# A second half product of each projection in seven block products, and the sums of h in one buffer, in a two-layer graph kernel on one core

## The chip, the cores and the metric

The kernel runs on one core of a Trainium2 chip. The metric is the device time of the whole kernel in microseconds (us), the median of several runs. Before the change it is 1522.22 us, the median of 3 runs (1521.25 to 1522.27). A core has five engines with a queue of instructions each: TensorE (PE; its weight loads are shown apart as PEld), VectorE (DVE), ScalarE (ACT), GpSimd (POOL) and SyncE (SP, which here issues the DMAs).

## What is computed

x is 128 x 128 x 512 (items, nodes, features), adj 128 x 128, all in fp32. Two layers follow each other; both are normalised ahead and added to x:

```python
h = relu(layernorm(x))
# layer 0: A = adj h, C = adj h + b;  max over n of relu(A[n'] + (C - A)[n]), so that
# what is left is relu(max_n A + b): one number for each item and node
x = x + layer0(h)
h = relu(layernorm(x))              # a number per node does not change a layernorm over features
q = h @ Wq + bq;  k = h @ Wk + bk;  v = h @ Wv + bv      # 8 heads of 64
w = softmax(q k^T / 8 + (0 where adj != 0, else -1e9))
x = x + w @ v
```

## The kernel before

**Groups.** The 128 items are worked on in 32 groups of four. The projections q, k and v of a group are products of 512 x 512 by 512 x 512 (four items of 128 nodes side by side). One turn of the main loop over g does, in this order on TensorE: `apply(g-1)` (weights by v, L600), `scores(g)` (q by k, L570), then the projection v of group g, and q and k of group g+1. Between their products stand the adjacency products of layer 0 (`adjacency`, L327) of later items. Everything else is put between these by hand: each projection is a list of steps, `part`, and `todo[s]` names what is issued right after step s. No scheduler reorders anything (`manual_schedule`); each engine does its instructions in the order in which the code issues them.

**A projection in seven products.** The class `Products` does a projection by a Strassen-Winograd scheme: weights and h are cut into quarters (a11 to a22, b11 to b22), four sums of weight quarters (s1 to s4, made once) and four of h quarters (t1 to t4, `h_sum`, L345, on VectorE for every group) are formed, and seven products of half size take the place of eight: p1 = a11 b11, p2 = a12 b21, p3 = s4 b22, p4 = a22 t4, p5 = s1 t1, p6 = s2 t2, p7 = s3 t3. Each is four matmuls of 128 x 128 weights by 256 columns into one PSUM bank (`mm`, L421). ScalarE copies p1 out with the bias (`biased`); VectorE adds p6 and p7 to it (u, L469, u3), and adds u and u3 to the banks of p5, p4 and p3 (`add`, L442), which gives the four quarters of the result. p2 is accumulated in the bank of p1 (bank a), which ScalarE copies to the first quarter, `dst(0, 0)`.

**Two of the seven in blocks.** In all projections but v of the first and last group and the k that is made ahead of the loop, p4 and p3 are done by the same scheme once more. `block_views` cuts their operands into blocks of 128; `h_blocks` (GpSimd, L359) makes four block sums of t4 and of b22 for each group, `weight_blocks` once those of a22 and s4. Each of the two products is then seven block products of 128 x 128 weights by 128 columns (`block_mm`, L487). Three of these go straight into the banks of p6/p7 and p5; four (numbers 1, 5, 6, 7) go to a scratch bank, 6, and are added into u by `more` (VectorE, L490). `p43a` does blocks 1 and 5, after p7; `p43b` does 6, the three direct ones and 7, after p5, and the last two adds.

**The steps of a turn.** Slots 0 to 5 are v (p1, p6, p2, p7 + p43a, p5, p43b), 6 to 11 are q, 12 to 17 k. The sums of h for group g+1 (`h_sum`) are in slots 0, 1, 2, 2 in a buffer of two (`hs`, pool `proj`), the block sums (`h_blocks`) in slots 5 and 6. `next_norms` places the normalisation of the next items: `norm` (bn_stats L279, aggregate L280, add eps L282 on VectorE, the power and a product on GpSimd, L284 and L286), `norm_end` (ScalarE, L289), `blocks` (32 x 32 transposes on VectorE, L302), `move` (16 DMAs that complete the transposition) and `add_bv` (GpSimd, L295). GpSimd also masks the exponentials (`mask`, L582) and adds the residual (L630).

What a step issues after its slot is two lines of the loop:

```python
for s, ps_ in enumerate(part):
    for p in ps_:
        p()
    for f, *args in todo[s]:
        f(*args)
```

Of the kernel before, what the change touches and what calls it, by code (L numbers as in the profile page):

```python
# [45 lines left out]
F32 = mybir.dt.float32  # L46
# [6 lines left out]
P = 128  # L53
G = 4
H, HD = 8, 64
# [112 lines left out]
def tile_adj_preln_d2(  # L168
# [14 lines left out]
    B, D, N = x.shape  # L183
# [4 lines left out]
    const = ctx.enter_context(tc.tile_pool(name="const", bufs=1))  # L188
# [1 line left out]
    W = {n: const.tile([P, NC, N], F32, name=f"w{n}_sb") for n in "qkv"}  # L190
    WS = {n: const.tile([P, 4, 2, N // 2], F32, name=f"s{n}_sb") for n in "qkv"}

    WB = {n: const.tile([P, 2, 4, P], F32, name=f"ss{n}_sb") for n in "qkv"}
    b0_sb = const.tile([P, 1], F32, name="b0_sb")
    bq_sb = const.tile([P, NC], F32, name="bq_sb")
    bk_sb = const.tile([P, NC], F32, name="bk_sb")
# [10 lines left out]
    def fast(ctx):  # L207
        xpool = ctx.enter_context(tc.tile_pool(name="xpool", bufs=7))
        proj = ctx.enter_context(tc.tile_pool(name="proj", bufs=2))
        one = ctx.enter_context(tc.tile_pool(name="one", bufs=1))  # L210
# [6 lines left out]
        X, HN, TB, HT, HB, H2, QT, KT, C, AMAX, WA, RSTD, NMR, PR = ({} for _ in range(14))  # L217

        def bank(k):

            return ps.tile([P, 512], F32, name=f"bk{k}")
# [109 lines left out]

        def h_quarters(g):
            t = HT[g]
            hs = proj.tile([P, 4, 2, 2, D], F32, name="hs")
            HB[g] = dict(
                b11=t[:, 0:2, 0:2], b12=t[:, 2:4, 0:2], b21=t[:, 0:2, 2:4], b22=t[:, 2:4, 2:4],
                **{f"t{k + 1}": hs[:, k] for k in range(4)},
            )
# [7 lines left out]

        def h_blocks(g, k):

            if k == 0:
                H2[g] = one.tile([P, 2, 4, D], F32, name="h2")  # L350
            b = HB[g]["b22 t4".split()[k]].rearrange("p t c d -> p c t d")
            t = H2[g][:, 1 - k]

            for o, x, y in (
                (t[:, 0:2], b[:, :, 1], b[:, 0]),
                (t[:, 2], b[:, 1, 1], t[:, 0]),
                (t[:, 3], b[:, 1, 0], t[:, 2]),
            ):
                nc.gpsimd.tensor_tensor(o, x, y, op=ALU.subtract)  # L359

        def weight_blocks(eng, n):

            for k in range(2):
                a = WA[n]["a22 s4".split()[k]].rearrange("p c (o f) -> p o c f", o=2)
                s = WB[n][:, k]
                for o, x, op, y in (
                    (s[:, 0], a[:, 1, 0], ALU.add, a[:, 1, 1]),
                    (s[:, 2], s[:, 0], ALU.subtract, a[:, 0, 0]),
                    (s[:, 1], a[:, 0, 0], ALU.subtract, a[:, 1, 0]),
                    (s[:, 3], a[:, 0, 1], ALU.subtract, s[:, 2]),  # L370
                ):
                    eng.tensor_tensor(o, x, y, op=op)
# [19 lines left out]
        class Products:  # L392
# [78 lines left out]
            def block_views(self):  # L471

                self.wa = [
                    WA[self.n][k].rearrange("p c (o f) -> p o c f", o=2) for k in ("a22", "s4")
                ]
                self.hb = [
                    HB[self.g][k].rearrange("p t c d -> p c t d") for k in ("t4", "b22")
                ]
                self.scr = bank(6).rearrange("p (m k d) -> p m k d", m=2, k=2)
                o_t = "(o d) -> p {} o t d" if self.n == "v" else "(t d) -> p {} o t d"  # L480
                r = "t" if self.n == "v" else "o"
                self.ub = self.u.rearrange(f"p k {r} " + o_t.format("k"), d=D)
                self.bk = lambda x: x.rearrange(f"p {r} " + o_t.format(""), d=D)

            def block_mm(self, out, w, h, start=False):
                lhs, rhs = (h, w) if self.n == "v" else (w, h)
                nc.tensor.matmul(out, lhs, rhs, start=start, stop=True, skip_group_check=True)  # L487

            def more(self, to, what):
                nc.vector.tensor_tensor(to, to, what, op=ALU.add)  # L490

            def p43a(self):

                self.block_views()
                s, t = WB[self.n], H2[self.g]
                for k in range(2):
                    self.block_mm(
                        self.scr[:, 0, k], self.wa[k][:, 0, 0], self.hb[k][:, 0, 0], start=k == 0
                    )
                for k in range(2):  # L500
                    self.block_mm(self.scr[:, 1, k], s[:, k, 0], t[:, k, 0])
                self.more(self.ub[:, :, 0, 0], self.scr[:, 0])
                for o in range(2):
                    self.more(self.ub[:, :, o, 1], self.scr[:, 1])
# [5 lines left out]

            def p43b(self):

                s, t, u, scr = WB[self.n], H2[self.g], self.ub, self.scr
                bc = [self.bk(self.b), self.bk(self.c)]
                for k in range(2):
                    self.block_mm(scr[:, 0, k], s[:, k, 2], t[:, k, 2])
                self.more(u[:, :, 0, 1], scr[:, 0])
                for k in range(2):
                    a, b = self.wa[k], self.hb[k]
                    self.block_mm(bc[k][:, 0, 0], a[:, 0, 1], b[:, 1, 0])  # L520
                    self.block_mm(bc[k][:, 0, 1], s[:, k, 3], b[:, 1, 1])
                    self.block_mm(bc[k][:, 1, 0], a[:, 1, 1], t[:, k, 3])
                for k in range(2):
                    self.block_mm(scr[:, 0, k], s[:, k, 1], t[:, k, 1])
                for i in range(2):
                    self.more(u[:, :, 1, i], scr[:, 0])
                self.add(self.dst(1, 0), self.b, self.u[:, 0])
                self.add(self.dst(0, 1), self.c, self.u[:, 1])

# [114 lines left out]
        def next_norms(m):  # L644

            return {
                0: [(norm_end, m, False), (norm_end, m + 1, False)],
                4: [(blocks, m)],
                6: [(blocks, m + 1), (move, m + 1), (add_bv, m), (add_bv, m + 1)], 7: [(adjacency, m)],
                8: [(norm, m + 2), (norm_end, m + 2)],  # L650
                12: [(norm, m + 3), (norm_end, m + 3), (adjacency, m + 1)],
                13: [(blocks, m + 2)],
                14: [(blocks, m + 3), (move, m + 3), (adjacency, m + 2)],
            }

        with tc.manual_schedule():
# [31 lines left out]
            k = Products(0, "k")  # L688
# [12 lines left out]
            for g in range(NG):  # L701
                b = g * G
# [2 lines left out]
                scores(g)  # L705
                part = []
                for p in [Products(g, "v")] + [Products(g + 1, n) for n in "qk" if g + 1 < NG]:
                    part += [[p.p1], [p.p6], [p.p2]]
                    if p.n == "v" and g in (0, NG - 1):
                        part += [[p.p7], [p.p5], [p.p4, p.p3]]  # L710
                    else:
                        part += [[p.p7, p.p43a], [p.p5], [p.p43b]]
                todo = {s: [] for s in range(len(part))}

                def add(s, *what):
# [2 lines left out]
                m = b + 2 * G  # L718
                if g + 1 < NG:
                    if g > 0:  # L720
                        for i in range(G):
                            residual(b - G + i, nc.gpsimd)
                    if m < B:
                        norm(m)
                        norm(m + 1)
                    if 0 < g < NG - 1:
                        add(0, adjacency, m - 1)
                    for k, s in enumerate((0, 1, 2, 2) if g > 0 else (3, 3, 4, 5)):
                        add(s, h_sum, g + 1, k)
                    for k, s in enumerate((5, 6)):  # L730
                        add(s, h_blocks, g + 1, k)
                    if g + 2 < NG:
                        for s, l in next_norms(m).items():
                            for what in l:
                                add(s, *what)
                    else:
                        add(6, count, 0, b)
                    eng = nc.gpsimd if m < B else nc.vector
                    at = (8, 9, 9, 10, 10, 13, 14, 15) if m < B else (4, 8, 8, 12, 12, 13, 14, 14)
                    for k, s in enumerate(at):  # L740
                        add(s, mask, eng, b + k // 2, k % 2)
                    if g + 2 < NG:
                        add(0, load, 2 * g + 5)
                    if g + 3 < NG:
                        add(8, load, 2 * g + 6)
                else:
                    for k, s in enumerate((0, 0, 0, 0, 2, 2, 3, 4)):
                        add(s, mask, nc.vector, b + k // 2, k % 2)
                    for i, s in enumerate((0, 0, 0, 1)):
                        add(s, residual, b - G + i)  # L750
# [13 lines left out]
            g = NG - 1  # L764
# [9 lines left out]
    with ExitStack() as c:  # L774
        fast(c)
# [35 lines left out]
```

## Time and profile before

The span of the profiled execution is 1519.2 us; the granted TensorE clock is 0.998 of full speed on average.

| engine | busy us | share | instructions |
|---|---|---|---|
| TensorE, matmuls | 1504.1 | 99% | 12909 |
| TensorE, weight loads | 1325.6 | 87% | 12909 |
| VectorE | 1023.2 | 67% | 2187 |
| ScalarE | 507.3 | 33% | 970 |
| GpSimd | 844.4 | 56% | 968 |

A middle group takes 46.75 us, and the groups are alike. In one of them, v takes 12.91 us of TensorE, q 12.62, k 13.57 (adjacency products included) and apply with scores 7.65; VectorE is busy for 7.71, 7.77, 8.96 and 7.18 of these.

Each matmul of fp32 shows as two instructions with two weight loads. Since matmuls are pipelined and their ends are modelled, a matmul's duration in the profile says less than the distance between the starts of two that follow each other. On the other engines an instruction's duration is what was measured, and one that follows without a wait starts a little before the end of the one ahead. A line of the timeline is: start, length, engine, line and operation, out<-in, partitions x elements and type, number of instructions merged; in brackets the idle time ahead of it and what ended it. A line of the groups is: line, engine, operation, out<-in, shapes, number, then busy us and mean ns of one, then idle us ahead of it and what ended it.

### The profile page before, as it was taken

The page shows a single profiled execution, that of the slowest core. Times are in us where ns is not written, and L with a number is a line of the kernel's source. Part 1 is how long each engine was busy: PE and PEld are TensorE (multiplying, and loading weights), DVE is VectorE, ACT ScalarE, POOL GpSimd, SP SyncE. Part 2 cuts the span into 40 slices and gives each one's busy share as a digit, 9 for nine tenths or more (in the row PEclk, how much of TensorE's full clock was granted, in tenths as well). Part 3 has the DMA queues.
Part 4 walks back from the last instruction along what each step waited for, and adds up shares of the span by engine and source line. Part 5 has one row for each costly group of instructions (what it writes and reads, how often), then busy time and mean ns, then how long its engine had stood idle before and what let it go on. Part 6 is the DMA issues. An engine that isn't in the chain of part 4 may idle for free.

```text
span 1519.2 us, 33036 instructions
## 1 busy us (share of the span) xinstructions
PE 1504.1 (99%) x12909; PEld 1325.6 (87%) x12909; DVE 1023.2 (67%) x2187; ACT 507.3 (33%) x970; POOL 844.4 (56%) x968
## 2 busy tenths in 40 slices
PE   8999999999999999999999999999999999999997
PEld 6888888888889888888888888888988888888886
DVE  6666666666666767666666666666676766666666
ACT  4333323333243332333332333324333233333232
POOL 5675656556565555654565655656555565456520
PEclk9999999999999999999999999999999999999999
DMA  5223222223222232222322222322223222222201
GB/s 170 58 65 80 59 65 74 65 76 75 52 73 67 73 83 43 76 66 74 80 58 65 75 65 76 73 54 73 66 73 84 43 76 76 64 80 57 52 32 58
DMA packets 307807, 105.32 MB, mean 69 GB/s; under 512 B 273153, under 2 KB 273281, under 8 KB 307649
## 3 DMA queue, kind: packets, MB, share of 16 engines
q1 hardware_dynamic: 307328, 102.84, 26.3%
q8 instruction: 104, 1.70, 0.5%
q14 instruction: 55, 0.44, 0.1%
q0 software_dynamic: 176, 0.27, 0.1%
q10 hardware_dynamic: 144, 0.07, 0.0%
HBM read 37.03 MB, written 33.55 MB: 46 GB/s over the span
## 4 chain that ended last, share of the span: by engine, by line
PE 99%; DVE 0%; DMA 0%; POOL 0%; ACT 0%; DVEq 0%; issue 0%
PE bk L421 55%; PE bk L487 19%; PE bk L600 8%; PE bk L570 8%; PE bk L327 7%; PE bk L546 1%; PE bk L321 0%; DMA xp<-in_x_dram 0%; DVE o L618 0%; ACT o L289 0%; DVE live L639 0%; DVE st L279 0%; DVE RS L617 0%; DVE o L630 0%; DVEq L776 0%; POOL rstd L284 0%
## 5 line engine op out<-in xcount | busy, mean ns | idle before, releaser
L630 POOL TENSOR_TENSOR o<-xp,o 128x512 f32<-128x512 f32 x122 | 151.1, 1268 | 312.7 <-DVE o L618 269.4
L582 POOL TENSOR_TENSOR w<-w,live 128x512 f32<-128x512 f32 x240 | 297.6, 1272 | 0.0
L490 DVE TENSOR_TENSOR u<-u,bk 128x256 f32<-128x256 f32 x552 | 205.7, 414 | 115.4 <-PE bk L487 111.3
L578 ACT ACTIVATE w<-bk 128x512 f32<-128x512 f32 x256 | 128.8, 625 | 345.6 <-PE bk L570 345.6
L295 POOL TENSOR_TENSOR xp<-xp,bv_sb 128x512 f32<-128x512 f32 x128 | 161.1, 1269 | 59.5 <-ACT hn L289 58.6
L421 PEld LDWEIGHTS bk<-hs,sk_sb 128*128 128x128 f32 x768 | 143.6, 190 | 44.7 <-issue 29.4
L421 PE MATMUL bk<-hs,sk_sb 128*128 128x256 f32 x768 | 181.3, 379 | 0.0
L421 PE MATMUL bk<-sv_sb,hs 128*128 128x256 f32 x768 | 181.2, 379 | 0.0
L421 PE MATMUL bk<-hs,sq_sb 128*128 128x256 f32 x744 | 175.8, 379 | 0.0
L421 PEld LDWEIGHTS bk<-sv_sb,hs 128*128 128x128 f32 x768 | 143.6, 190 | 31.1 <-issue 14.3
L328 DVE TENSOR_REDUCE amax<-bk 128x1 f32<-128x512 f32 x128 | 88.2, 689 | 105.4 <-PE bk L327 102.5
L359 POOL TENSOR_TENSOR h<-hT 128x256 f32<-128x256 f32 x31 | 22.6, 728 | 238.2 <-PE bk L487 233.8
L421 PEld LDWEIGHTS bk<-hs,sq_sb 128*128 128x128 f32 x744 | 138.9, 190 | 17.7
L469 DVE TENSOR_TENSOR u<-bk,u 128x512 f32<-128x512 f32 x95 | 65.8, 692 | 116.7 <-PE bk L421 114.6
L289 ACT ACTIVATE hn<-xp,nmr,rstd 128x512 f32<-128x512 f32 x124 | 100.8, 813 | 104.8 <-POOL nmr L286 104.8
L327 PE MATMUL bk<-hn,adjT 128*128 128x512 f32 x248 | 126.6, 592 | 0.0
L600 PE MATMUL bk<-v,w 128*64 128x65 f32 x4096 | 126.5, 222 | 0.0
L600 PEld LDWEIGHTS bk<-v,w 128*64 128x64 f32 x4096 | 122.1, 137 | 4.1 <-issue 0.3
L421 PE MATMUL bk<-wv_sb,hT 128*128 128x256 f32 x512 | 124.3, 386 | 0.0
L570 PE MATMUL bk<-qT,kT 64*128 64x128 f32 x2048 | 122.9, 275 | 0.0
L421 PE MATMUL bk<-hT,wk_sb 128*128 128x256 f32 x512 | 121.2, 380 | 0.0
L570 PEld LDWEIGHTS bk<-qT,kT 64*128 64x128 f32 x2048 | 116.8, 188 | 2.5 <-issue 0.3
(149 smaller groups left out, 2575.1 us busy)
## 6 DMA issues: line engine op xcount, KB each, us to landing
out_dram<-o SPq DMA_DIRECT2D x128, 256.0 KB, 2.0
xp<-in_x_dram SPq DMA_DIRECT2D x62, 512.0 KB, 3.9
hT<-tb SPq DMA_DIRECT2D x992, 32.0 KB, 1.9
xp<-in_x_dram SPq DMA_DIRECT2D x4, 256.0 KB, 4.4
wq_sb<-in_L_gnn_Wq_dram SPq DMA_DIRECT2D x2, 512.0 KB, 8.2
wk_sb<-in_L_gnn_Wk_dram SPq DMA_DIRECT2D x2, 512.0 KB, 9.8
wv_sb<-in_L_gnn_Wv_dram SPq DMA_DIRECT2D x2, 512.0 KB, 10.5
bv_sb<-in_L_gnn_bv_dram POOLq DMA_DIRECT2D x1, 256.0 KB, 6.7
```

Source lines behind the costliest of these rows:

```text
L289: nc.scalar.activation(HN[m], x_of(m), AF.Relu, scale=RSTD[m], bias=NMR[m])
L295: nc.gpsimd.tensor_tensor(x_m, x_m, bv_sb, op=ALU.add)
L327: nc.tensor.matmul(pa, adjT, HN[m], start=True, stop=True)
L328: nc.vector.reduce_max(AMAX[g][:, i : i + 1], pa, axis=AX.X)
L421: nc.tensor.matmul(bank[:, r, :], lhs, rhs, start=first and r == 0 and c == 0, stop=r == 1 and c == 1, skip_group_check=True,)
L487: nc.tensor.matmul(out, lhs, rhs, start=start, stop=True, skip_group_check=True)
L490: nc.vector.tensor_tensor(to, to, what, op=ALU.add)
L570: nc.tensor.matmul(psc[j][:, f, :], KT[g][r, f, i * D : (i + 1) * D], QT[g][r, f, i * D : (i + 1) * D], start=True, stop=True,)
L578: nc.scalar.activation(w[:, j], psc[j], AF.Exp, scale=HD ** -0.5)
L582: eng.tensor_tensor(w[:, j], w[:, j], live_h, op=ALU.mult)
L600: nc.tensor.matmul(pav[r, c : c + HE], w[:, h % 2, h // 2, r], V[:, i, h, :], start=True, stop=True,)
L630: eng.tensor_tensor(y, x_of(b), y, op=ALU.add)
```

## The change

p2 is done in seven block products too, by the same scheme as p4 and p3, in the projections that use blocks. For that:

- `weight_blocks` makes block sums of a12 as well, once; `h_blocks` those of b21, for each group, in a tile of its own for each of the three operands.
- p2 becomes three steps. `p2a`, in place of p2: blocks 1 and 5 go to the two quarters `sum2` and `five` of a spare bank (2 for q, else 5), the three direct ones into bank a; ScalarE copies bank a to `dst(0, 0)` as before, and VectorE adds `sum2` and `five` into it (`more2`). `p2b`, after p7: block 6 into `sum2`, and one sum. `p2c`, after p43a: block 7 into `sum2`, and one sum.
- `hs` has one buffer in place of two (this makes room for the new tiles). The sums for group g+1 then can't be written while v of group g reads the old ones, so `h_sum` moves to slots 5, 5, 6, 6, and `h_blocks` to 5 (b21, b22) and 6 (t4).
- The last sums of v (`p43c`) are issued at slot 6, ahead of q's p1, behind the first two of these.
- `blocks` of the next two items move from slots 4 and 6 to 1 and 2, their `move` from 6 to 5.

It is for TensorE: four matmuls of 256 columns become seven of 128.

```diff
-    WB = {n: const.tile([P, 2, 4, P], F32, name=f"ss{n}_sb") for n in "qkv"}
+    WB = {n: const.tile([P, 3, 4, P], F32, name=f"ss{n}_sb") for n in "qkv"}
...
-            hs = proj.tile([P, 4, 2, 2, D], F32, name="hs")
+            hs = one.tile([P, 4, 2, 2, D], F32, name="hs")
...
-            b = HB[g]["b22 t4".split()[k]].rearrange("p t c d -> p c t d")
-            t = H2[g][:, 1 - k]
+            b = HB[g]["t4 b22 b21".split()[k]].rearrange("p t c d -> p c t d")
+            t = H2[g, k] = one.tile([P, 4, D], F32, name=f"h2{k}")
...
+            def p2a(self):
+
+                self.block_views()
+                x = bank(2 if self.n == "q" else 5)
+                self.sum2, five = x[:, 0:D], x[:, D : 2 * D]
+                self.block(self.sum2, 2, 1)
+                self.block(five, 2, 5)
+                self.blocks_in(self.bk(self.a), 2)
+                self.biased(self.dst(0, 0), self.a, 0)
+                self.more2(0, 0, self.sum2)
+                self.more2(slice(0, 2), 1, five)
+
+            def p2b(self):
+                self.block(self.sum2, 2, 6)
+                self.more2(0, 1, self.sum2)
+
+            def p2c(self):
+                self.block(self.sum2, 2, 7)
+                self.more2(1, slice(0, 2), self.sum2)
...
-                4: [(blocks, m)],
-                6: [(blocks, m + 1), (move, m + 1), (add_bv, m), (add_bv, m + 1)], 7: [(adjacency, m)],
+                1: [(blocks, m)], 2: [(blocks, m + 1)],
+                5: [(move, m + 1)], 6: [(add_bv, m), (add_bv, m + 1)], 7: [(adjacency, m)],
...
-                    part += [[p.p1], [p.p6], [p.p2]]
                     if p.n == "v" and g in (0, NG - 1):
-                        part += [[p.p7], [p.p5], [p.p4, p.p3]]
+                        part += [[p.p1], [p.p6], [p.p2], [p.p7], [p.p5], [p.p4, p.p3]]
                     else:
-                        part += [[p.p7, p.p43a], [p.p5], [p.p43b]]
+                        part += [
+                            [p.p1], [p.p6], [p.p2a], [p.p7, p.p2b, p.p43a, p.p2c], [p.p5],
+                            [p.p43b, p.p43c],
+                        ]
+                        if p.n == "v":
+                            late = part[-1].pop()
+                    if p.n == "q" and g > 0:
+                        part[6].insert(0, late)
...
-                    for k, s in enumerate((0, 1, 2, 2) if g > 0 else (3, 3, 4, 5)):
+                    for k, s in enumerate((5, 5, 6, 6)):
                         add(s, h_sum, g + 1, k)
-                    for k, s in enumerate((5, 6)):
+                    for k, s in ((2, 5), (1, 5), (0, 6)):
                         add(s, h_blocks, g + 1, k)
```

More of the change, by code (lines that the diff above doesn't have):

```diff
@@ L347, in h_blocks @@
         def h_blocks(g, k):
-            if k == 0:
-                H2[g] = one.tile([P, 2, 4, D], F32, name="h2")
-            b = HB[g]["b22 t4".split()[k]].rearrange("p t c d -> p c t d")
-            t = H2[g][:, 1 - k]
+            b = HB[g]["t4 b22 b21".split()[k]].rearrange("p t c d -> p c t d")
+            t = H2[g, k] = one.tile([P, 4, D], F32, name=f"h2{k}")
             for o, x, y in (
@@ L361, in weight_blocks @@
         def weight_blocks(eng, n):
-            for k in range(2):
-                a = WA[n]["a22 s4".split()[k]].rearrange("p c (o f) -> p o c f", o=2)
+            for k in range(3):
+                a = WA[n]["a22 s4 a12".split()[k]].rearrange("p c (o f) -> p o c f", o=2)
                 s = WB[n][:, k]
@@ L473, in block_views @@
                 self.wa = [
-                    WA[self.n][k].rearrange("p c (o f) -> p o c f", o=2) for k in ("a22", "s4")
+                    WA[self.n][k].rearrange("p c (o f) -> p o c f", o=2)
+                    for k in ("a22", "s4", "a12")
                 ]
                 self.hb = [
-                    HB[self.g][k].rearrange("p t c d -> p c t d") for k in ("t4", "b22")
+                    HB[self.g][k].rearrange("p t c d -> p c t d") for k in ("t4", "b22", "b21")
                 ]
-                self.scr = bank(6).rearrange("p (m k d) -> p m k d", m=2, k=2)
+                self.s = WB[self.n]
+                self.t = [H2[self.g, k] for k in range(3)]
                 o_t = "(o d) -> p {} o t d" if self.n == "v" else "(t d) -> p {} o t d"
@@ L487, in block_mm, with blocks_in, block @@
                 nc.tensor.matmul(out, lhs, rhs, start=start, stop=True, skip_group_check=True)
+            def blocks_in(self, bank, k):
+                a, b, s, t = self.wa[k], self.hb[k], self.s[:, k], self.t[k]
+                self.block_mm(bank[:, 0, 0], a[:, 0, 1], b[:, 1, 0])
+                self.block_mm(bank[:, 0, 1], s[:, 3], b[:, 1, 1])
+                self.block_mm(bank[:, 1, 0], a[:, 1, 1], t[:, 3])
+            def block(self, out, k, m):
+                if m == 1:
+                    self.block_mm(out, self.wa[k][:, 0, 0], self.hb[k][:, 0, 0], start=k != 1)
+                else:
+                    e = {5: 0, 6: 2, 7: 1}[m]
+                    self.block_mm(out, self.s[:, k, e], self.t[k][:, e])
@@ L489, in more, with more2 @@
             def more(self, to, what):
                 nc.vector.tensor_tensor(to, to, what, op=ALU.add)
-            def p43a(self):
[L494 to L501, printed above, removed]
+            def more2(self, o, t, what):
+                d = self.dst(0, 0)
+                if self.n == "v":
+                    d = d.rearrange("p t (o h) d -> p o t h d", o=2)
+                    what = what.rearrange("p (h d) -> p h d", d=HD)
+                else:
+                    d = d.rearrange("p o (t d) -> p o t d", t=2)
+                to = d[:, o, t]
+                if len(to.shape) > len(what.shape):
+                    what = what.unsqueeze(1).to_broadcast(to.shape)
+                self.more(to, what)
@@ L502, in p43a @@
+            def p2c(self):
+                self.block(self.sum2, 2, 7)
+                self.more2(1, slice(0, 2), self.sum2)
+            def p43a(self):
+                self.scr = bank(6).rearrange("p (m k d) -> p m k d", m=2, k=2)
+                for m in (1, 5):
+                    for k in range(2):
+                        self.block(self.scr[:, m // 5, k], k, m)
                 self.more(self.ub[:, :, 0, 0], self.scr[:, 0])
@@ L511, in p43b, with p43c @@
             def p43b(self):
-                s, t, u, scr = WB[self.n], H2[self.g], self.ub, self.scr
-                bc = [self.bk(self.b), self.bk(self.c)]
                 for k in range(2):
-                    self.block_mm(scr[:, 0, k], s[:, k, 2], t[:, k, 2])
-                self.more(u[:, :, 0, 1], scr[:, 0])
+                    self.block(self.scr[:, 0, k], k, 6)
+                self.more(self.ub[:, :, 0, 1], self.scr[:, 0])
+                for k, x in enumerate((self.b, self.c)):
+                    self.blocks_in(self.bk(x), k)
                 for k in range(2):
[L519 to L524, printed above, removed]
+                    self.block(self.scr[:, 0, k], k, 7)
+            def p43c(self):
                 for i in range(2):
-                    self.more(u[:, :, 1, i], scr[:, 0])
+                    self.more(self.ub[:, :, 1, i], self.scr[:, 0])
                 self.add(self.dst(1, 0), self.b, self.u[:, 0])
```

## The prediction

> **What bounds the kernel now.** I read the page's shares by engine and its chain first. The chain that ended last runs on TensorE for 99% of the span, 55% at the full products (L421), 19% at the block products (L487).
>
> ```profile
> PE 99%; DVE 0%; DMA 0%; POOL 0%; ACT 0%; DVEq 0%; issue 0%
> PE bk L421 55%; PE bk L487 19%; PE bk L600 8%; PE bk L570 8%; PE bk L327 7%; PE bk L546 1%; PE bk L321 0%; DMA xp<-in_x_dram 0%; DVE o L618 0%; ACT o L289 0%; DVE live L639 0%; DVE st L279 0%; DVE RS L617 0%; DVE o L630 0%; DVEq L776 0%; POOL rstd L284 0%
> ```
>
> So a microsecond of TensorE removed is gained and one of waiting is lost. Next, the timeline of TensorE in a middle group: the q projection, then the one place in v where TensorE waits.
>
> ```profile
> 718.28 1.89 PE L421 MATMUL bk<-hT,wq_sb 128*128 128x256 f32 x8
> 720.01 1.89 PE L421 MATMUL bk<-hs,sq_sb 128*128 128x256 f32 x8
> 721.74 0.38 PE L487 MATMUL bk<-hs,wq_sb 128*128 128x128 f32 x2
> 721.96 0.39 PE L487 MATMUL bk<-hT,sq_sb 128*128 128x128 f32 x2
> 722.18 0.61 PE L487 MATMUL bk<-h,ssq_sb 128*128 128x128 f32 x4
> 722.63 1.89 PE L421 MATMUL bk<-hs,sq_sb 128*128 128x256 f32 x8
> ...
> 713.11 0.39 PE L487 MATMUL bk<-sv_sb,h 128*128 128x128 f32 x2
> 713.42 0.71 PE L487 MATMUL bk<-ssv_sb,h 128*128 128x128 f32 x4
> 713.97 1.89 PE L421 MATMUL bk<-hT,wq_sb 128*128 128x256 f32 x8
> ```
>
> Starts count here, since ends overlap: p2 at 718.28, p7 at 720.01, so a full product takes 1.73; four blocks take 722.63 - 721.74 = 0.89, so a block 0.222. In v's line at 713.42 TensorE waits for VectorE. The timeline of VectorE shows for what:
>
> ```profile
> 712.36 0.70 DVE L302 STREAM_TRANSPOSE tb<-hn 128x512 f32<-128x512 f32 x1
> 712.99 0.38 DVE L490 TENSOR_TENSOR u<-u,bk 128x256 f32<-128x256 f32 x1
> ```
>
> The sum was queued behind a transpose and ended at 713.37. The blocks were due at 713.11 + 0.22 = 713.33, the product after them at 713.78; it came at 713.97. So a wait costs **end of the VectorE instruction + 0.16 - time due**. Then the groups by shape, for prices:
>
> ```profile
> L490 DVE TENSOR_TENSOR u<-u,bk 128x256 f32<-128x256 f32 x552 | 205.7, 414 | 115.4 <-PE bk L487 111.3
> L469 DVE TENSOR_TENSOR u<-bk,u 128x512 f32<-128x512 f32 x95 | 65.8, 692 | 116.7 <-PE bk L421 114.6 <-ACT hn L289 2.1
> L302 DVE STREAM_TRANSPOSE tb<-hn 128x512 f32<-128x512 f32 x124 | 83.7, 694 | 2.4 <-ACT hn L289 2.4
> L436 ACT ACTIVATE qT<-bk,bq_sb 128x256 f32<-128x256 f32 x62 | 26.0, 471 | 82.6 <-PE bk L421 82.6
> ```
>
> Instructions that follow each other start about 0.08 before the end of the one ahead: 512 elements take steps of 0.61 and 256 steps of 0.33 (three L490 in 1.08). L490's x552 says 92 projections use blocks (six sums each): 30 of v, 31 each of q and k.
>
> [...] the sum at 712.99 stood behind a transpose it had nothing to do with, and TensorE stood with it. [...] A block here is two passes, each with its load, in 2 x 111 ns; [...] and seven of them aren't seven eighths of 1.73 (1.51) but 1.56. [...] blocks 6 and 7 of p2, written to the bank half `sum2`, wait also for the sum that reads the other half, `five`.
>
> **The change, part by part.**
>
> *Matmuls.* p2 falls from 1.73 to 7 x 0.222 = 1.56: -0.17 for each of 92, -15.6 us.
>
> *Transposes moved* out of v's p5 to slots 1 and 2: the wait at 713.42 goes, -0.19 x about 30 = -5.7.
>
> *Four sums more for each projection* (more2): two of 128 elements, two of 256. No row shows 128; between L469 and L490 the slope is 1.09 ns an element, so 0.28 long, in steps of 0.20 ([...] lower bound 0.20, a reciprocal of 7 elements out of PSUM at L617). VectorE gets 1.07 x 92 = 98 us more on its 1023: no bound as a sum, but it's the order that counts. By the order of the built program, p2 writes blocks 1 and 5 to a spare bank and the others to bank a (p2a); then come p7, block 6 into `sum2` (p2b), four blocks of p43a, block 7 into `sum2` (p2c), p5. **Block 6 waits until both first sums have read the bank; block 7 until block 6 is added.** Behind each of them stands everything on TensorE. On VectorE block 6's sum stands behind p7's u3 sum, and that behind what the slot before holds.
>
> q, from the end of p2a on TensorE. Block 7 is due at 1.73 + 0.22 + 0.89 = 2.84. ScalarE's two bias copies start at 0.20 (in the trace: 720.21 after 720.01) and end at 1.04, the second sum starts at 1.08; the norm (bn_stats, aggregate, add) follows at 1.41 and takes a step of 1.07 (728.78 to 729.85 in the timeline); u3 at 2.48; block 6's sum at 3.09 to 3.37; block 7 at 3.53. **Lost: 0.69.** Block 6, due at 1.73 with its sums over at 1.49, loses nothing.
>
> v, on the clock above. p2a ends at 705.48 + 5 x 0.222 = 706.59, block 6 is due at 708.32. But ScalarE normalises x of m+1 until 707.35 in the trace of before, held by GpSimd, so the copy of v stays at 707.40 to 707.99; the sums run from 708.03 and 708.23 to 708.64, block 6 at 708.80: lost 0.48. A transpose follows at 708.56, u3 at 709.19, block 6's sum at 709.80 to 710.08; block 7, due at 709.91, comes at 710.24: lost 0.33. **Lost: 0.81.**
>
> k. An adjacency product (0.86) after p2a puts block 7 at 3.70. GpSimd is later than before (below), so that ScalarE's normalisation of m+3 ends 0.50 after p2a: copies 0.54 to 1.38, second sum 1.42, transpose 1.75, reduction 2.38, u3 2.99, block 6's sum 3.60 to 3.88, block 7 4.04. **Lost: 0.34**; if ScalarE is free, nothing.
>
> *h in quarters in one buffer.* The sums h_sum must wait for the last block of v that reads them, and h_sum 0 and 1 then stand ahead of v's last sums, which is what p43c is held back for. From v's p43b (2.22 long): the last reader ends about 1.1 in, h_sum 1 is over at 2.4; q's p6, which wants it, is due at 2.22 + 1.73 = 3.95. Hidden by p1, with 1.5 to spare. t3 and t4 follow by 5.7, wanted at 8 (p7).
>
> *A third h_blocks* costs GpSimd 0.73 + 2 x 0.48 = 1.7 a group: 53 us on 844, no bound. It also waits for t4, now late, so the norm of m+3 comes about 1.6 later; the masks end near 37.4 after v's p1, wanted from 40 on. Hidden, but for the ScalarE delay in k.
>
> *A third weight_blocks*: four small sums a weight, at the start, under 1 us once on VectorE. Moves at slot 5: the queue of DMAs waits, nobody for it.
>
> **Sum.** v 0.81 - 0.17 - 0.19 = +0.45; q 0.69 - 0.17 = +0.52; k 0.34 - 0.17 = +0.17. 0.45 x 29 + 0.52 x 31 + 0.17 x 31 = +34.4 (the second to last group has no norms, so about 0 for v). 1522.2 + 34 = 1556. Without k's delay (-10.5): 1546. With the 128-element sums at 0.20 in place of 0.28 (about 0.08 in each of the three waits): 7 less, so 1539 at the low end.
>
> **Rivals.** (1) *The sums hide and TensorE gets its saving*: 1522.2 - 15.6 - 5.7 = 1501. For it: VectorE idles for 0.65 to 1.8 at a time in the slots concerned. Against: the idle time lies behind the waits for p7 and p5, not where the sums fall. (2) *Half of the waiting*: if VectorE starts sums closer together or copies end earlier, 1.84 a group becomes 0.9, and saving and waiting cancel to about +0.2 a group: 1528; a little less gives no change. (3) *Waits pile up*: GpSimd's delay reaches the masks or h20, as much as 0.5 to 1 a group more: 1575 or so. Against: 2.5 us to spare in the masks, about 2 in h20.
>
> **How the numbers follow.** Forecast 0.70 (1556); rival 1 0.09; rival 2 0.12; rival 3 0.09. Range 1534 to 1574: the forecast with its bounds, and the upper part of rival 2 and most of rival 3. Faster by over 0.2%: rival 1 and a sliver of 2, 0.10. Within: 0.03. Slower: 0.87.
>
> **What would show it.** In the profile after, TensorE's starts: 0.7 of nothing ahead of the single block between p43a and p5 in q, about 0.3 in k, 0.5 and 0.3 in v; the weight loads at L487 idle 50 us or so, by VectorE sums; a group of 47.9 instead of 46.75. A prediction of waits is wrong if those starts are 0.11 to 0.22 apart throughout; the prices are wrong if the gaps are there but of other lengths.

## The result, and the profile after

The changed kernel takes 1531.84 us (median, 1531.65 to 1532.05) against 1521.88 us for the kernel before: a ratio of 1.0066, 95% interval 1.0048 to 1.0083. It is slower, as forecast, but by 10 us and not by 34, and 2 us below the range. The span of the profile went from 1519.2 to 1530.0 us.

The shares by engine and the first line of its chain, after:

```profile
PE 1502.0 (98%) x13461; PEld 1335.5 (87%) x13461; DVE 1121.5 (73%) x2559; ACT 501.0 (33%) x970; POOL 886.2 (58%) x1069
PE 18%; DVE 2%; SPq 1%; DMA 1%; issue 0%; POOL 0%; ACT 0%; DVEq 0%
```

VectorE got 98.3 us more, as forecast (98). TensorE's share fell by a point: it waits more. The chain has lost its thread here (its parts are 22% of the span), so the timelines have to do its work. TensorE in q of the same middle group; the kernel before had no gap in this stretch:

```profile
725.77 1.89 PE L419 MATMUL bk<-hs,sq_sb 128*128 128x256 f32 x8
...
728.17 0.61 PE L487 MATMUL bk<-h,ssq_sb 128*128 128x128 f32 x4
729.12 0.49 PE L487 MATMUL bk<-h,ssq_sb 128*128 128x128 f32 x2 [0.34 <-DVE qT L505]
729.45 1.89 PE L419 MATMUL bk<-hs,sq_sb 128*128 128x256 f32 x8
```

p7 starts at 725.77, which is the end of p2a. With 1.73 for p7, 0.22 for block 6, 0.89 for four blocks and 0.22 for block 7, p5 was due at 728.835; it started at 729.45. **q loses 0.615**, ahead of block 7 (the line at 729.12, held by VectorE's L505). The bracket's 0.34 is less than the loss: it counts from the modelled end of the line before (728.78), not from 728.61, when block 7 was due. So starts have to be compared. What VectorE did meanwhile:

```profile
726.48 0.79 DVE L505 TENSOR_TENSOR qT<-qT,bk 128x128 f32<-128x128 f32 x2 [0.93 <-ACT qT L434]
727.18 0.69 DVE L279 BATCH_NORM_STATS2 st<-xp 128x6 f32<-128x512 f32 x1
...
728.19 0.68 DVE L467 TENSOR_TENSOR u<-bk,u 128x512 f32<-128x512 f32 x1
728.79 0.28 DVE L505 TENSOR_TENSOR qT<-qT,bk 128x128 f32<-128x128 f32 x1
```

Block 6's sum (728.79) stands behind u3 (728.19), and that behind the norm (from 727.18): it ends at 729.07. Block 7 starts 0.05 later and takes 0.33 to the next start instead of 0.22, so the product behind it starts 0.38 after that end: the 0.22 of a block, and 0.16 more. Now v, TensorE, where two waits were forecast:

```profile
713.17 1.90 PE L419 MATMUL bk<-sv_sb,hs 128*128 128x256 f32 x8
714.90 0.39 PE L487 MATMUL bk<-ssv_sb,h 128*128 128x128 f32 x2
...
716.38 1.89 PE L419 MATMUL bk<-sv_sb,hs 128*128 128x256 f32 x8
```

Block 6 starts at 714.90 = 713.17 + 1.73, on time. Only block 7 is late: the product after it was due at 716.235 and came at 716.38. **v loses 0.145**, not 0.81. In k, from p7 to p5:

```profile
739.70 1.89 PE L419 MATMUL bk<-hs,sk_sb 128*128 128x256 f32 x8
...
742.89 1.89 PE L419 MATMUL bk<-hs,sk_sb 128*128 128x256 f32 x8
```

The same reading (with the third decimals of the trace) gives 742.89 for 742.755: **0.135**, not 0.34. The groups by shape answer to those of before:

```profile
L505 DVE TENSOR_TENSOR u<-u,bk 128x256 f32<-128x256 f32 x552 | 206.2, 415 | 88.6 <-PE bk L487 88.4
L487 PE MATMUL bk<-h,ssq_sb 128*128 128x128 f32 x558 | 95.6, 280 | 10.3 <-DVE qT L505 10.3
```

The sum costs what it did (415 ns for 414), and q's blocks are the ones that wait: 10.3 us by VectorE's sums, about 0.34 in each of 30 projections, as in the timeline.

A middle group takes 46.96 instead of 46.75. The waits, 0.145 + 0.615 + 0.135 = 0.895, less the saving of three p2 (3 x 0.168) and of the wait at v's end (0.19), are +0.20: the group is accounted for.

### The profile page after: what moved, and what is told of

The parts are those of the page before. It is cut to its first block, busy times and chain, and to the rows that moved or that the text cites. A ratio compares the mean times of both kernels' runs of the same rounds, so it can differ in the third digit from the quotient of the medians.

```text
span 1530.0 us, 34887 instructions
## 1 busy us (share of the span) xinstructions
PE 1502.0 (98%) x13461; PEld 1335.5 (87%) x13461; DVE 1121.5 (73%) x2559; ACT 501.0 (33%) x970; POOL 886.2 (58%) x1069
## 5 line engine op out<-in xcount | busy, mean ns | idle before, releaser
L505 DVE TENSOR_TENSOR u<-u,bk 128x256 f32<-128x256 f32 x552 | 206.2, 415 | 88.6 <-PE bk L487 88.4
L357 POOL TENSOR_TENSOR h<-hT 128x256 f32<-128x256 f32 x62 | 45.7, 737 | 187.7 <-PE bk L487 187.3
L487 PE MATMUL bk<-h,ssq_sb 128*128 128x128 f32 x558 | 95.6, 280 | 10.3 <-DVE qT L505 10.3
L659 DVE TENSOR_TENSOR o<-bk,RS 128x448 f32<-128x448 f32 (+1 forms) x161 | 93.6, 582 | 7.2
L487 PEld LDWEIGHTS bk<-h,ssq_sb 128*128 128x128 f32 x558 | 81.6, 191 | 19.5 <-DVE qT L505 16.1
```

Of the source, the lines that this page charges most:

```text
L659: nc.vector.tensor_tensor(oo, po[:, :, 0:HD], rs.unsqueeze(2).to_broadcast([P, rs.shape[1], HD]), op=ALU.mult,)
```

## The experiments

Three questions were open: does the saving exist at all, is it the waits for the shared bank that eat it, and why does v wait so much less than worked out?

**The rearrangement alone.** All of the change stays, except that p2 is whole again:

```diff
- [p.p1], [p.p6], [p.p2a], [p.p7, p.p2b, p.p43a, p.p2c], [p.p5],
+ [p.p1], [p.p6], [p.block_views, p.p2], [p.p7, p.p43a], [p.p5],
```

> The rearrangement alone: p2 is again one product of four matmuls, all else of the change stays (h sums in one buffer behind v, late p43c, transposes at slots 1 and 2). Theory (the waits of block 7 for VectorE cost what the blocks of p2 save, and more): no wait for block 7, and v's wait of 0.19 behind the transpose is gone, so 1522 - 0.19 x 29 = 1516, plus about 3 once (q's p6 in group 0 waits 0.7 for the late h sums, the second to last group 2.2 behind the count on VectorE): 1518 to 1520. Rival (h sums in one buffer and their late place are what costs): stays near 1530.

1518.13 us, ratio 0.9976 (0.9967 to 0.9986), a group of 46.56: exactly 46.75 - 0.19. With the transposes moved out of v's end, no wait is left there, which is what was forecast. The third set of block sums and the h sums in one buffer cost a middle group nothing.

**Block 7 in a bank of its own**, so that it doesn't wait until block 6 is added. The kernel leaves out blocks 1 and 6 in the second row of that quarter, which shared the bank with block 7.

```diff
- self.block(self.sum2, 2, 7)
- self.more2(1, slice(0, 2), self.sum2)
+ seven = bank(0 if self.n == "q" else 3)[:, 0:D]
+ # block 7 as before, but out=seven, start=True
+ self.more2(1, slice(0, 2), seven)
```

> Block 7 of p2 goes to a bank of its own (0 for q, 3 for v and k), so that it need not wait for block 6's sum; VectorE has the same work in the same order. Theory: the waits of 0.61 (q), 0.14 (v) and 0.13 (k) go, 19 + 4 + 4 = 27: 1504, faster than both kernels. Rival (TensorE is held by VectorE's 98 us of new sums as such, and the wait comes back at the next instruction that needs VectorE, in p5 or p43b): 1525 to 1532.

1507.14 us, ratio 0.9907 (0.989 to 0.9923), a group of 46.08. That is 46.75 - 0.19 - 3 x 0.168 = 46.06: all of the saving and no wait left. The one wait for block 6's sum is what the change loses in q, k and v.

With one more sum of 256 elements, so that nothing is left out:

> The run with block 7 of p2 in a bank of its own left out a part: in one bank, block 7 adds up on blocks 1 and 6, which the second row of the result needs, and in a bank of its own it doesn't; so that row lacked them. Here VectorE adds the bank half with blocks 1 and 6 to that row too, one sum of 256 elements more for each projection (92 x 0.33 = 31 us of VectorE). Theory (what isn't ahead of a wait of TensorE costs nothing): as without it, 1506 to 1510. Rival (VectorE's load as such costs): 1520 or more.

1510.43 us, ratio 0.9922 (0.9905 to 0.9938), a group of 46.21, 0.4 us over what was expected. VectorE does even more here than in the changed kernel, and none of the three waits is left. Of the group, 0.13 comes back in k: a block that goes to p5's bank waits until VectorE has read p5, and the sum added stands ahead of that. So here VectorE's load costs only where something on TensorE waits behind it.

**The norm a slot earlier** in q, so that u3 and block 6's sum stand behind it no longer:

```diff
- 7: [(adjacency, m)], 8: [(norm, m + 2), (norm_end, m + 2)],
+ 7: [(adjacency, m), (norm, m + 2)], 8: [(norm_end, m + 2)],
```

> The norm of item m+2 on VectorE moves from slot 8 of q to slot 7, ahead of p2's sums instead of between them and p7's sum. Theory (block 7 waits for what is queued on VectorE ahead of block 6's sum): q's wait falls from 0.61 to about 0.1, 0.5 x 30 = 15 less: 1516 to 1518. Rival (the wait is the time of the sums themselves, whatever is between): 1530 to 1532.

A miss: 1526.13 us, ratio 1.0027 (1.0016 to 1.0038). q's wait fell from 0.615 to 0.10 as expected, but k's rose from 0.135 to 0.38. ScalarE in k shows why:

```profile
734.44 0.81 ACT L289 ACTIVATE hn<-xp,nmr,rstd 128x512 f32<-128x512 f32 x1 [1.88 <-POOL nmr L286]
735.16 0.82 ACT L434 ACTIVATE kT<-bk,bk_sb 128x256 f32<-128x256 f32 x2
```

p2a's end is the adjacency product's start, 734.49. k's copies stand behind a normalisation that GpSimd released late (`nmr`): without q's wait TensorE ends p2a 0.48 earlier in the group than in the changed kernel, but GpSimd's power, behind five masks, starts only 0.20 earlier. So the copies begin 0.67 after p2a, where they begin 0.40 after it in the changed kernel. I had forecast such a delay for the change itself; here it came.

**Why v waits so little.** The forecast kept ScalarE's copy of v at its place in the trace of before. The lines of VectorE, GpSimd and ScalarE there (v's first product starts at 701.06):

```profile
705.05 0.69 DVE L345 TENSOR_TENSOR hs<-hT 128x512 f32<-128x512 f32 x1
705.13 1.01 POOL L284 TENSOR_TENSOR rstd<-ve,mhalf 128x1 f32<-128x1 f32 x1
706.54 0.81 ACT L289 ACTIVATE hn<-xp,nmr,rstd 128x512 f32<-128x512 f32 x1 [0.52 <-POOL nmr L286]
707.40 0.59 ACT L432 COPY v<-bk 128x512 f32<-128x512 f32 x1
```

And after (v's first product at 707.64):

```profile
711.71 0.55 POOL L284 TENSOR_TENSOR rstd<-ve,mhalf 128x1 f32<-128x1 f32 x1
711.79 1.68 ACT L289 ACTIVATE hn<-xp,nmr,rstd 128x512 f32<-128x512 f32 x2 [1.49 <-POOL nmr L286]
713.38 0.58 ACT L430 COPY v<-bk 128x512 f32<-128x512 f32 x1
```

GpSimd's second power of 128 x 1 elements took 1.01 before and takes 0.55 after. ScalarE's second normalisation then follows the first without the wait of 0.52, and v's copy ends 6.32 after the start of v instead of 6.93. What had stood beside the 1.01 was `h_sum` 0, a VectorE sum with both operands in SBUF, and the change moves that sum to behind v. To test it, one such subtraction is put into the changed kernel at slot 0 of v; in a second kernel it has the same size, and reads one operand from PSUM:

```diff
+ if 0 < g < NG - 2: add(0, extra, g + 1)
...
  # both in SBUF
+ nc.vector.tensor_sub(o, t[:, 2:4, 0:2], t[:, 0:2, 0:2])
  # or one in PSUM (p: the bank of the adjacency product)
+ nc.vector.tensor_sub(o, t[:, 2:4, 0:2], p)
```

> Added: in slot 0 of v, where h_sum 0 stood before the change, VectorE does one more subtraction of 128x512 with both operands in SBUF, written to a dead part of qT (it is used nowhere). VectorE is idle there, so its 0.6 costs nothing by itself. Theory (VectorE's h_sum stretched GpSimd's power for the norm from 0.55 to 1.0 us in the kernel before; with h_sum moved away ScalarE's copy of v's p2 came 0.6 earlier than forecast, and v's block 6 did not wait): the longest power instruction is back at about 1.0, v's block 6 waits 0.2 to 0.5, and the time rises by 6 to 14: 1538 to 1546. Rival (the power was slow for another reason): power 0.55, time as the changed kernel, 1530 to 1533.

> As the run with the added subtraction in slot 0 of v, but one of its two operands is the adjacency product in PSUM; the same size, place and output (used nowhere). Theory (two operands in SBUF are what hinders GpSimd): longest power instruction about 0.6, v's waits as in the changed kernel, 1530 to 1534. Rival (any work of VectorE at that moment hinders it): longest power instruction 1.0, 1540 to 1546 as with both operands in SBUF.

Both operands in SBUF: 1544.12 us, ratio 1.0149 (1.0132 to 1.0166), a group of 47.42, v's waits 0.31 and 0.28. One in PSUM: 1531.83 us, ratio 1.0066 (1.0049 to 1.0082), a group of 46.95, the changed kernel's. The timelines, first with both in SBUF:

```profile
717.22 0.69 DVE L350 TENSOR_TENSOR qT<-hT 128x512 f32<-128x512 f32 x1
717.31 1.01 POOL L284 TENSOR_TENSOR rstd<-ve,mhalf 128x1 f32<-128x1 f32 x1
...
719.44 0.56 ACT L435 COPY v<-bk 128x512 f32<-128x512 f32 x1
```

and with one in PSUM:

```profile
710.95 0.69 DVE L351 TENSOR_TENSOR qT<-hT,bk 128x512 f32<-128x512 f32 x1
711.04 0.55 POOL L284 TENSOR_TENSOR rstd<-ve,mhalf 128x1 f32<-128x1 f32 x1
```

The same 0.69 of VectorE, the same place, 0.09 ahead of the power: 1.01 or 0.55. So it is the sum's two operands in SBUF that make the power long, not VectorE's work as such. In the lines above the power ends 0.40 after the sum does (705.74 to 706.14, 717.91 to 718.32). The kernel before has 28 such groups: the power starts 0.08 to 0.11 behind `h_sum` 0, takes 0.99 to 1.02 and ends 0.40 to 0.41 after it. In one more (1079.13) it starts 0.27 ahead of that sum and takes 0.55. What the two engines share there isn't shown.

The counterpart is the kernel before with `h_sum` 0 put in slot 1:

```diff
- for k, s in enumerate((0, 1, 2, 2) if g > 0 else (3, 3, 4, 5)):
+ for k, s in enumerate((1, 1, 2, 2) if g > 0 else (3, 3, 4, 5)):
```

> The kernel before, with only h_sum 0 moved from slot 0 to slot 1, out of the way of GpSimd's second power instruction of the norm. Theory: that one falls from 1.0 to 0.55 and ScalarE's normalisation and its copy of v's p2 begin at once (copy still behind p2's end); TensorE did not wait for either, so the time is that of the kernel before, 1520 to 1523. Rival (the long power instruction is the second of a pair, whatever VectorE does): it stays at 1.0.

1522.3 us in the one run made, a group of 46.75 as before, no power over 0.60 us, and the two normalisations are one stretch:

```profile
706.11 1.68 ACT L289 ACTIVATE hn<-xp,nmr,rstd 128x512 f32<-128x512 f32 x2 [1.49 <-POOL nmr L286]
708.29 0.59 ACT L432 COPY v<-bk 128x512 f32<-128x512 f32 x1 [0.51 <-PE bk L421]
```

So the 0.46 by which the power was longer was there in the kernel before, and harmless: v's copy starts 6.34 after v's first product (701.95 here), as it does with the long power, and here it waits 0.51 for the end of p2. With blocks the long power costs v most of what was forecast: in the kernel with the subtraction put back v loses 0.59, four times the 0.145.

**Block 6's sum ahead of u3.** If block 7 waits for that sum, only VectorE's order need change: u3 is issued after p2b (`p7b` is the u3 sum).

```diff
- [p.p1], [p.p6], [p.p2a], [p.p7, p.p2b, p.p43a, p.p2c], [p.p5],
+ [p.p1], [p.p6], [p.p2a], [p.p7, p.p2b, p.p7b, p.p43a, p.p2c], [p.p5],
```

> Only the order on VectorE is changed: p7's sum u3 comes after block 6's sum instead of ahead of it; the same instructions on all engines, and block 7 still waits for block 6's sum. Theory (the wait is what VectorE has queued ahead of that sum): block 6's sum comes 0.6 earlier, the waits of q, v and k fall from 0.61, 0.14, 0.13 to 0.02, 0 and about 0.1 (k's copies stand behind GpSimd's chain, which doesn't move up): a group 46.2, 1506 to 1510. Rival (block 7's wait for a sum that itself waits for block 6 costs the round trip whatever is queued): at most half of it, 1520 or more.

1512.22 us, ratio 0.9939 (0.9923 to 0.9956), a group of 46.21 as expected; the median is 2 us over the range. The repetition, beside the last kernel of this part:

> The order alone once more, beside the run above on the same chip: 1508 to 1513, group 46.2.

1512.07 us, ratio 0.9934 (0.9917 to 0.995). In the two profiles group 1 takes 48.37 and 50.09, the second to last 46.18 and 47.86; what these two lose comes below. TensorE and VectorE in q, in the first profile:

```profile
717.41 0.84 PE L489 MATMUL bk<-h,ssq_sb 128*128 128x128 f32 x6
717.43 0.28 DVE L507 TENSOR_TENSOR qT<-qT,bk 128x128 f32<-128x128 f32 x1
717.63 0.68 DVE L469 TENSOR_TENSOR u<-bk,u 128x512 f32<-128x512 f32 x1
718.09 1.89 PE L419 MATMUL bk<-hs,sq_sb 128*128 128x256 f32 x8
```

The six are three blocks, the last of them block 7, due at 717.41 + 0.45 = 717.86. The sum ends at 717.71, in time, and the product follows 0.68 after 717.41: nothing waits. v's wait is gone too; k's 0.13 is left, which is what keeps the group from 46.06.

**What happens once.** Group 1 of the changed kernel takes 48.62 and the second to last 47.04, where before they took 46.75 and 44.58. TensorE in v of group 1, and VectorE in q of the second to last:

```profile
104.23 0.49 PE L487 MATMUL bk<-ssv_sb,h 128*128 128x128 f32 x2 [1.10 <-DVE v L505]
```

```profile
1476.77 1.56 DVE L681 SCALAR_TENSOR_TENSOR tb<-RS,tb 128x960 f32<-128x960 f32 x1
...
1478.26 0.68 DVE L458 TENSOR_TENSOR u<-bk,p1a 128x512 f32<-128x512 f32 x1
```

In group 1 block 6 waits for v's copy, late because GpSimd, which makes the weights' block sums of v, now makes four more of them (0.41 each) ahead of a residual and the norms. In the second to last, the u sum of q stands behind `count` (L681, 1.56), and p7 waits 2.17 for it. A first try moved `count` to slot 10 of q and the weights' sums to VectorE at slots 3, 4 and 10 of group 0:

> The order with block 6's sum ahead of u3, and two things that cost once: the count of the second to last group goes from slot 6 to slot 10 on VectorE (behind it stood q's p6 sum, and TensorE waited 2.2 for it), and the block sums of v's weights move from GpSimd at the end of group 0 to VectorE in its slots 3, 4 and 10 (GpSimd was late for group 1's norms by them). Theory: 2 to 4 less than the 1512 of that order alone: 1507 to 1510. Rival (the time there was set by something else): 1511 to 1513.

1510.65 us, ratio 0.9932 (0.9916 to 0.9949), a miss: group 1 fell to 46.20 and the second to last to 45.48, but group 0 took 51.78. VectorE and TensorE in q of group 0:

```profile
71.65 0.28 DVE L370 TENSOR_TENSOR ssv_sb<-wv_sb 128x128 f32<-128x128 f32 x1
...
73.12 1.34 DVE L370 TENSOR_TENSOR ssv_sb<-wv_sb 128x128 f32<-128x128 f32 x1
76.12 0.94 PE L489 MATMUL bk<-h,ssq_sb 128*128 128x128 f32 x4 [3.34 <-DVE u L507]
```

The same, the other way round: the first sum, which started 0.03 ahead of GpSimd's first mask (71.68), took 0.28, the three that fell beside the masks, which also have both operands in SBUF, 1.24 to 1.35, about the length of a mask (1.28). The second try puts the sums in slots 2, 3 and 4, and `count` ahead of v:

```diff
+ if g + 2 == NG:
+     count(0, b)
...
- add(15, weight_blocks, nc.gpsimd, "v")
+ for k, s in enumerate((2, 3, 4)):
+     add(s, weight_blocks, nc.vector, "v", (k,))
```

> As the last try of it, with the one-time work in other places: the count of the second to last group goes ahead of its v, where VectorE is idle for 4.7 us, and the block sums of v's weights go to VectorE in slots 2, 3 and 4 of group 0, where each is followed by an idle microsecond. Theory: group 0 as with the order alone (46.6), group 1 46.2 instead of 48.4, the second to last 2.2 to 2.9 shorter: 4 to 5 less than the order alone on the same chip: about 1507. Rival (waits move elsewhere, as in the try with slot 10, where 3.5 us came up in group 0): no more than 2 less.

1504.42 us (1503.63 to 1505.33), ratio 0.989 (0.9873 to 0.9906), faster than both kernels. Groups 1 to 29 take 46.21, but for three that take 0.1 to 0.2 more; the second to last takes 44.11. It does all of the change's work, and 0.54 x 29 = 15.7 of the 17.3 by which its span is shorter than before come from the middle groups.

## Why the prediction was right in direction and wrong in size

What the forecast said of a middle group, and what the trace after has (us, for each group; saved is negative):

| | forecast | measured |
|---|---|---|
| three p2 in blocks, each | -0.17 | -0.168 |
| wait at v's end gone | -0.19 | -0.19 |
| q waits for block 6's sum | 0.69 | 0.615 |
| v waits, block 6 | 0.48 | 0 |
| v waits, block 7 | 0.33 | 0.145 |
| k waits | 0.34 | 0.135 |
| sum | +1.14 | +0.20 |

**The matmuls, the sums, the formula: right.** The saving came to the hundredth (46.56 and 46.08), block sums of 128 elements took 0.28 as estimated, and the formula gives the product behind block 7 again: in k the sum ends at 742.51, with 0.16 and a block of 0.22 the product comes at 742.89, as it did. Only the reason for 1.56 in place of 1.51 isn't shown: the passes of 128, 256 and 512 columns start 0.111, 0.216 and 0.429 apart, nearly in proportion, and their weight loads are recorded with 0.19 each, overlapping. Rival 1, for the middle groups, is what the kernel with block 7 in a bank of its own shows; the changed kernel had these 0.895 us of waits instead.

**The step that failed is v's**: "ScalarE normalises x of m+1 until 707.35 in the trace of before, held by GpSimd, so the copy of v stays at 707.40 to 707.99". It took over two things from the trace of before that the change itself undoes.

- It names GpSimd as what holds ScalarE, and takes the 1.01 us of the power as given. But these 1.01 were made by `h_sum` 0 beside it, and the same change moves `h_sum` out of that place, which the forecast priced two paragraphs later as "hidden". With such a sum put back, v loses 0.59; without it, 0.145. That is 0.445 x 29 = 12.9 us of the forecast, and the two kernels are 12.3 us apart.
- It takes 707.40 as the time from which ScalarE is free. But there the copy waited for p2 too: p2 ends at 707.20 (the start of p7), and a copy follows a product by 0.20. The kernel before with `h_sum` 0 moved shows it: normalised earlier, copied at the same 6.34. With p2 in blocks and the long power the copy starts at 6.21 (719.44), and is 0.03 shorter. This and smaller steps behind it are the rest between 0.81 and 0.59: 0.22 x 29 = 6.4 us.

So in the changed kernel the copy ended 0.61 earlier than forecast, block 6's wait went and block 7's shrank: 0.81 became 0.145, 0.665 x 29 = 19.3 us too much.

**q was mis-sized by 0.075**: u3 came 1.01 after the norm's start and not 1.07, the rest is rounding; 2.3 us. **k by 0.205**: the normalisation of m+3 ends 0.49 after p2a, as forecast (0.50), but ScalarE starts its copies 0.09 before that end and not 0.04 after it (0.40 for 0.54); what follows on VectorE comes earlier by that and by a step a little shorter than worked out (reduction to u3 0.57 for 0.61), and block 6's sum ends 3.67 after p2a instead of 3.88. 6.4 us.

**The once-costs were set too low**, "under 1 us once": group 0 +1.2, group 1 +1.9 and the second to last +2.5, of which the regular part explains 0.2 each at most. The start adds 1.05 and the end takes 1.86 back. The sum by spans: 1.05 (start) + 1.2 (group 0) + 1.87 (group 1) + 6.1 (groups 2 to 29) + 2.46 (second to last) - 1.86 (end) = 10.8. The start's 1.05 isn't the change's: by the distances between its starts (the passes of an adjacency product 0.85 apart, later 0.43) TensorE runs at half speed up to 10.5 us in the profile before and up to 12.9 in that after, and in the two profiles of block 6's sum ahead of u3, one and the same kernel, up to 10.9 and 12.4, with 0.6 between their first starts of v. The end's 1.86 lies behind TensorE's last product: about 5 us are left there in every kernel here with p2 in blocks, 6.9 to 7.2 in the three with p2 whole; its cause is open.

So 19.3 + 2.3 + 6.4 = 28 us of waits too many, less some 4 us that came up outside the middle groups, is the 24 by which the forecast was off. The direction hung on q: without its 0.615 a group would have gained 0.41. What happened is rival 2: half of the waiting (0.895 of 1.84), saving and waiting cancel to +0.2 a group, copies that end earlier; it had 0.12. Rival 3, a pile-up, had nothing for it.

## What to carry to other kernels

A duration that is taken over from the trace of before holds only if what stood beside it stays there: before using it, look whether it is longer than the others of its line (1.01 where the median of 128 is 0.55), ask what made it so, and whether the change moves that. Where two block products share a bank, the sum between them belongs at once behind its product, ahead of any sum that is wanted later; that order alone was worth 20 us here. And a change in every turn of a loop is priced by its turn, but the first and last turns have other neighbours and have to be priced on their own.

## What the runs showed of the hardware that I had not expected

- A GpSimd instruction on one element a partition, 0.55 us, takes 0.99 to 1.02 in the kernel before where a VectorE sum of 512 elements with both operands in SBUF has started 0.08 to 0.11 earlier, and up to 1.09 in the kernel with such a subtraction put back. Beside one of the same length with an operand in PSUM it takes 0.55, and none of the 128 of that kernel takes more than 0.62. VectorE's sums of 128 elements grow from 0.28 to 1.24 to 1.35 beside GpSimd's masks.
- A stretch of half speed on TensorE followed some stalls of 2.0 to 2.3 us, and not others. In the kernel with block 7 in a bank of its own, block 6 of v came 2.28 late in group 1, and the next product took 2.69 from start to start instead of 1.73:

```profile
104.03 0.49 PE L487 MATMUL bk<-ssv_sb,h 128*128 128x128 f32 x2 [2.11 <-DVE v L505]
...
106.17 2.85 PE L419 MATMUL bk<-sv_sb,hs 128*128 128x256 f32 x8
108.86 0.61 PE L487 MATMUL bk<-ssv_sb,h 128*128 128x128 f32 x4
```

  The granted clock was 0.50 from 104.69 to 108.10 us and 1.00 behind it. In the changed kernel the stall of 2.17 in the second to last group was followed by 1.00 (1478.90 to 1484.00). Of the kernel with block 6's sum ahead of u3 there are two profiles. In the first (granted clock 0.999 on average), stalls of 2.04 in group 1 and of 2.17 in the second to last group were followed by full speed; in the second (0.997), stalls of 2.09 and 2.17 at the same places by 3.41 us at 0.50 each, and the two groups took 1.7 us more each. These 3.4 us are most of what lies between the fastest and the slowest run of this kernel (1508.3 and 1512.9). So one and the same wait cost 1.7 us more than its length in one run and not in the other, and a median can lie on either side of that; which stall is followed by half speed isn't shown.
